# Graph transformer on one core: two value groups and two tail steps per turn beside the longest block

## Chip, cores and metric

The kernel runs on one core of a Trainium2 chip. The metric is the device time of one execution in microseconds (us); five executions of the kernel before gave 2874.62, 2865.3, 2837.87, 2857.81 and 2864.56, with a median of 2864.56. The core has five engines with instruction queues of their own: TensorE (PE, with its weight loads shown as PEld), VectorE (DVE), ScalarE (ACT), GpSimd (POOL) and SyncE (SP, which issues DMAs). Semaphores order them against each other; within one queue the work goes in the order in which it is written.

## What is computed

3327 nodes with 256 features, and a dense 0/1 adjacency of 3327 x 3327 in which a node has some 16 neighbours. Layer 0 averages over the neighbours, with softmax weights, and normalises. Then three layers, each of them the same graph transformer layer, sparse by the adjacency:

```python
qkv = layer_norm(x, g1, be1) @ w_qkv              # 8 heads of 32
scores = einsum('nhd,mhd->hnm', q, k) * SCALE
attn = softmax(where(adj != 0, scores, -inf))
out = einsum('hnm,mhd->nhd', attn, v).reshape(n, 256)
x = x + out @ w_proj + b_proj
h2 = layer_norm(x, g2, be2)
x = x + gelu(h2 @ w1 + b1) @ w2 + b2              # hidden width 1024
```

## The kernel before

Layer 0 works on the dense adjacency; on the way it sorts the nodes by their number of neighbours and lists the neighbours of each. It ends near 410 us and the change does not touch it. The three sparse layers (layer 1 to about 1275 us, layer 2 to 2082, layer 3 to the end) are what follows.

*Blocks and slots.* The nodes stand in 26 blocks of 128, one node to a partition. `CAPS[b]` says how many neighbours (slots) block b has room for: 34 in block 0, 23 and 22 in blocks 1 and 2, down to 9 in block 25. A slot of a block is one indirect DMA (L767, issued by GpSimd), which fetches the key and value rows of 128 neighbours. Up to `SG` = 4 slots form a group with one tile: block 0 has 9 groups, block 1 and block 2 have 6, block 25 has 3. Twelve such tiles exist (`SLOTS`), and gathers are sent up to `AHEAD` = 3 groups ahead of the scores.

*Order.* `ORDER` is 24, 23, ..., 1, 0, 25: blocks with few slots first, the longest (block 0) last but one, the shortest last. `CHUNKS` pairs them for the work behind the attention: [23,24], [21,22], ..., [3,4], [1,2], and block 0 and block 25 by themselves.

*The loop of a layer* (L879 on) goes through the blocks, k = 0 to 25, and through the groups g of each. One pass sends gathers, computes the scores of the group (`scores`: a product L781 and a sum L782 on DVE), after the last group also the maximum and the exponentials (`exps`, L788 to L792), then calls `turn()`. Then comes the block before: at g = 0 its softmax shares (`shares`, L798 to L800), and in each group as many of its value groups as `goal` says (`values`: a product L812 on DVE, then transposes on PE that sum up in `po`, L815). When all value groups of a chunk are through (a copy to oT on ACT, L821), the chunk's *tail* is opened. So the shares of block 0 and its value groups are written among the scores of block 25 (k = 25), and those of block 1 among the scores of block 0 (k = 24).

*A tail* is a generator, and `turn()` moves each open tail on by one step, the oldest first. Its steps, by lines: projection on PE (L666, L670; `pp`); add to x and variances on DVE (L673, L132 to L135); powers on POOL (L139); normalisation (L151 on DVE, L155 on ACT); transposes on PE and copy on ACT (L165, L167; `fT`); first half of the hidden layer on PE with gelu on ACT (L694, L698; `pu`); its products with the second matrix (L707; `pd`); second half of `pu`; second half of `pd`; add to x on DVE (L713) and variances; powers; normalisation; transposes (`hT`); and for each block of the chunk keys, values and queries of the next layer (L185 `pk`, L190 `pq`, copied by ACT at L187 and L192, and stored by SP at L729 and L730). The last layer has no such rows: after L713 the blocks are ready to be written to the output by POOL (L833). The list `hidden` lets one tail at a time into the MLP steps.

*At the end of a layer.* Beside block 25 (k = NB - 1, the last) `turn()` is called twice in a group. After the loop `turn()` goes on until no tail is left: the drain. The next layer's gathers wait for the stored rows of all blocks.

*What sets the order.* All of it stands under a manual schedule: each engine's queue holds the instructions in the order in which `layer` writes them. No planner changes it.

In the kernel before, chunk [3,4] is in its MLP beside the first groups of block 0; chunk [1,2] gets its projection beside block 0's group 6, its transposes and the first MLP steps beside block 25, and the rest in the drain together with the tails of [0] and [25].

Of the kernel before, what the change touches and what calls it, by code (L numbers as in the profile page):

```python
# [31 lines left out]
NB = (N + P - 1) // P  # L32
# [34 lines left out]
def kernel(ctx: ExitStack, tc: tile.TileContext, ins, out: bass.AP):  # L67
    nc = tc.nc

    def wt(L, name):  # L70
        return ins[f"L{L}_gnn_{name}"]
# [34 lines left out]
    def load_wq(L):  # L106
        t = wq_pool.tile([P, 2, 3 * D], FP, tag="wq", name=f"wq{L}")
        nc.scalar.dma_start(t, wt(L, "w_qkv").rearrange("(c p) n -> p c n", p=P))
        return t
# [87 lines left out]
    def node_rows(b):  # L197

        if b not in nodes_:
            nodes_[b] = lists.tile([P, NODE], FP, tag="node", bufs=NODES, name=f"node_{b}")  # L200
        nc.gpsimd.indirect_dma_start(
            out=nodes_[b], out_offset=None, in_=node_dr[:, :],
            in_offset=bass.IndirectOffsetOnAxis(ap=perm[:, b:b + 1], axis=0))
# [8 lines left out]
    def node_list(b):  # L212

        t = nodes_[b]
        cd = t[:, 2 * D:2 * D + CAND]
        nr = (CAPS[b] + 7) // 8
        w = 8 * nr

        cg = lists.tile([P, CAND], FP, tag="cg", bufs=2, name=f"cg_{b}")
        nc.vector.scalar_tensor_tensor(cg, cd, 0.0, segb.rearrange("p s k -> p (s k)"), ALU.is_gt, ALU.mult)  # L220
        nc.vector.tensor_add(cg, cg, cd)
        ls = lists.tile([P, LW], FP, tag="ls", bufs=2, name=f"ls_{b}")
        for k in range(nr):
            nc.vector.max(out=ls[:, 8 * k:8 * k + 8], in_=cg)
            if k < nr - 1:
                nc.vector.match_replace(out=cg, in_to_replace=ls[:, 8 * k:8 * k + 8], in_values=cg, imm_value=0.0)
        em = lists.tile([P, LW], FP, tag="em", bufs=2, name=f"em_{b}")
        own = lists.tile([P, 1], FP, tag="own", bufs=1, name=f"own_{b}")
        nc.vector.tensor_scalar(em[:, :w], ls[:, :w], 0.5, None, ALU.is_lt)
        nc.vector.tensor_scalar(own, pf[:, b:b + 1], 1.0, None, ALU.add)  # L230
        nc.vector.scalar_tensor_tensor(ls[:, :w], em[:, :w], own, ls[:, :w], ALU.mult, ALU.add)
        nc.vector.tensor_scalar(idx[:, b, :w], ls[:, :w], -1.0, None, ALU.add)
        nc.vector.tensor_scalar(bias[:, b, :w], em[:, :w], NEG, None, ALU.mult)
        nc.vector.tensor_reduce(found[:, b, 0:1], em[:, :w], AX.X, ALU.add)
        nc.scalar.copy(found[:, b, 1:2], t[:, 2 * D + CAND:])


    with ExitStack() as st:
# [51 lines left out]
        for L in LAYERS:  # L290
            o = 16 * (L - 1)
            for k, name in ((0, "g1"), (2, "be1"), (4, "g2"), (6, "be2"), (8, "b1")):
                n = wt(L, name).shape[0] // P
# [337 lines left out]
    with ExitStack() as st:  # L631
# [15 lines left out]
        def node_x(b):  # L647
            nc.scalar.copy(x_sb[:, b, :], nodes_[b][:, :D])

        def load_weights(L):  # L650
            w = {}
            for name, c, n in (("w_proj", 2, D), ("w1", 2, FF), ("w2", 8, D)):
                w[name] = wts.tile([P, c, n], FP, tag=name, name=f"{name}_{L}")
                nc.sync.dma_start(w[name], wt(L, name).rearrange("(c p) n -> p c n", p=P))
            return w
# [173 lines left out]
        def write(most):  # L829

            for b in ended[:most]:
                r = ROWS[b]
                nc.gpsimd.indirect_dma_start(  # L833
                    out=out, out_offset=bass.IndirectOffsetOnAxis(ap=perm[:r, b:b + 1], axis=0),
                    in_=x_sb[:r, b, :], in_offset=None)
            del ended[:most]

        def turn():

            for e in list(tails):  # L840
                e[0] -= 1
                if e[0] <= 0:
                    e[0] = next(e[1], None)
                    if e[0] is None:
                        tails.remove(e)

        def layer(L):
            w = load_weights(L)
            wqn = load_wq(L + 1) if L < LAYERS[-1] else None
            att = [Attend(L, b) for b in ORDER]  # L850
            todo = [(a, g) for a in att for g in range(len(a.cuts))]
            turns = len(todo)
            held = 0
            sent = 0
            oTs = {}
            left = [len(c) for c in CHUNKS]
            first = L == LAYERS[0]
            if first:
                for b in ORDER[:EARLY]:
                    node_rows(b)  # L860
                    node_x(b)
            att[0].load_q()
            att[0].place_q()
            att[1].load_q()
            att[1].place_q()
            before = None

            def part(a):

                m, j = place[a.b]  # L870
                if m not in oTs:
                    oTs[m] = work.tile([P, 2, 2 * P], FP, tag="oT", name=f"oT_{L}_{m}")
                if a.values(oTs[m], j):
                    left[m] -= 1
                    if not left[m]:
                        tails.append([1, tail(L, w, wqn, CHUNKS[m], oTs.pop(m))])

            now = 0
            for k, a in enumerate(att):  # L879
                n = len(a.cuts)  # L880
                if k + 2 < NB:
                    att[k + 2].load_q()
                for g in range(n):
                    if first and g == 0:
                        if k + EARLY < NB:
                            node_rows(ORDER[k + EARLY])
                        if EARLY <= k + 2 < NB:
                            node_list(ORDER[k + 2])
                            node_x(ORDER[k + 2])
                    while sent < turns and held < SLOTS and sent - now <= AHEAD:  # L890
                        todo[sent][0].gather(todo[sent][1])
                        sent += 1
                        held += 1
                    a.scores(g)
                    if g == n - 1:
                        a.exps()

                        if k + 2 < NB:
                            att[k + 2].place_q()
                    turn()  # L900
                    if k == NB - 1:
                        turn()
                    if sent == turns or len(ended) > LATE:
                        write(1)
                    if before is not None:
                        if g == 0:
                            before.shares()
                        goal = max(g + 1, -(-len(before.cuts) * (g + 1) // max(n - 1, 1)))
                        while before.vdone < min(goal, len(before.cuts)):
                            part(before)  # L910
                            held -= 1
                    now += 1
                before = a
            before.shares()
            while before.vdone < len(before.cuts):
                part(before)
                turn()
                write(1)
            while tails:
                turn()  # L920
                write(1)
            write(NB)

        with tc.manual_schedule():
            for L in LAYERS:
                layer(L)
# [190 lines left out]
```

## Time and profile before

| | us |
|---|---|
| median of 5 executions | 2864.56 (2837.87 to 2874.62) |
| profiled execution | 2858.64 |
| its span | 2856.8 |
| mean granted TensorE clock in it | 0.749 |
| layer 2: scores of block 0, group 1 (L781) | 1971.65 |
| layer 2: shares of block 0 (L798) | 2010.67 |
| layer 2: first `pu` of block 0, of block 25 | 2049.85, 2063.12 |
| layer 2: first gather of layer 3 | 2082.07 |
| layer 1: shares of block 0; first `pu` of block 0, of block 25 | 1202.73; 1242.99, 1256.26 |
| layer 3: shares of block 0; first `pu` of block 0, of block 25 | 2789.08; 2823.63, 2832.22 |

All times below the first line are of the profiled execution, counted from the start of its span. A line of a timeline reads: start, length, engine, line of the kernel, operation, output from inputs, shape, how many in a row, and in brackets how long the engine had been idle and who released it. "DVE L713 x_sb<-x_sb,pd [6.18 <-PE pd L707]" is the add that closes an MLP, which waited 6.18 us for PE. A group line of the page adds up all instructions of one line: count, busy us and mean ns, then the idle time just before them and what ended it.

### The profile page before, as it was taken

Reading aid. Unit: us, or ns where it says so; the run is one execution under the profiler, and the core shown is the slowest. Engines: PE = TensorE matmul, PEld = TensorE weight load, DVE = VectorE, ACT = ScalarE, POOL = GpSimd, SP = SyncE. Lnnn points to the kernel's source line nnn. Section 1 sums busy time; section 2 is a strip of 40 time slices with the busy share of each in tenths; the row PEclk is TensorE's granted clock in tenths of the full one; section 3 lists DMA queues with packets and bytes.
Section 4 is the critical chain, followed back from the end, with each engine's and each line's share of the span. In section 5 each row is a group of like instructions: output and inputs, shape, how many; then the busy total and the mean of one; then the engine's idle time right before and its main releaser. Section 6 shows DMA issues by size and latency. Waiting matters only on the chain.

```text
span 2856.8 us, 26111 instructions
## 1 busy us (share of the span) xinstructions
PE 1718.3 (60%) x8346; PEld 1331.5 (47%) x8346; DVE 1754.6 (61%) x3214; ACT 777.3 (27%) x1564; POOL 1430.6 (50%) x1614
## 2 busy tenths in 40 slices
PE   7677621455676666672556766766824556665656
PEld 6555411344554444451445544554613444454545
DVE  4877744676567776724654667657445757755573
ACT  4777510122332222230122222222311222111112
POOL 0232336565456665416554556656164656665562
PEclk8888855777787666795677878777956778676778
DMA  5667255455455664526554555656174655555561
GB/s 185 231 188 220 65 125 178 139 173 167 123 157 176 179 180 147 148 85 200 148 172 133 158 165 179 200 168 183 45 230 126 177 157 169 173 164 155 151 180 43
DMA packets 165083, 453.05 MB, mean 159 GB/s; under 512 B 37711, under 2 KB 64985, under 8 KB 161609
## 3 DMA queue, kind: packets, MB, share of 16 engines
q0 software_dynamic: 107104, 350.26, 41.8%
q1 hardware_dynamic: 56652, 98.53, 10.8%
q10 hardware_dynamic: 1180, 2.49, 0.3%
q8 instruction: 69, 1.13, 0.2%
q14 instruction: 78, 0.64, 0.1%
HBM read 410.86 MB, written 40.29 MB: 158 GB/s over the span
## 4 chain that ended last, share of the span: by engine, by line
PE 36%; another core or an unknown queue 16%; DVE 15%; issue 15%; ACT 6%; DMA 5%; POOL 5%; DVEq 0%; SPq 0%; ACTq 0%; POOLq 0%
PE pd L707 8%; PE pu L694 8%; PE po L815 6%; PE pk L185 5%; DVE sl L781 3%; POOL sl L767 3%; DVE sl L812 3%; PE pp L670 2%; PE pq L190 2%; DVE sc L782 2%; DMA sl<-kv,idx 2%; DMA kv<-kvr 1%; DMA node<-qr 1%; DVE cand L610 1%
## 5 line engine op out<-in xcount | busy, mean ns | idle before, releaser
L767 POOL DMA_INDIRECT sl<-kv,idx x1290 | 1228.9, 953 | 564.0 <-issue 358.6
L815 PE MATMUL po<-ident,sl 128*128 128x128 f32 x2580 | 470.2, 346 | 580.5 <-DVE sl L812 315.0
L815 PEld LDWEIGHTS po<-ident,sl 128*128 128x128 f32 x2580 | 396.0, 180 | 645.0 <-DVE sl L812 348.7
L781 DVE TENSOR_TENSOR sl<-sl,qw 128x1024 f32<-128x1024 f32 (+1 forms) x354 | 396.0, 1119 | 82.4 <-ACT qw L760 43.0
L782 DVE TENSOR_REDUCE sc<-sl 128x32 f32<-128x1024 f32 (+1 forms) x354 | 398.2, 1125 | 37.3 <-remote 20.1
L694 PE MATMUL pu<-fT,w 128*128 128x256 f32 (+1 forms) x1344 | 327.6, 401 | 137.5 <-ACT fT L167 89.3
L812 DVE TENSOR_TENSOR sl<-sl,qw 128x1024 f32<-128x1024 f32 (+1 forms) x354 | 388.9, 1119 | 9.1 <-remote 3.4
L707 PE MATMUL pd<-w,gT 128*128 128x256 f32 x1248 | 329.8, 421 | 107.2 <-ACT gT L698 73.1
L694 PEld LDWEIGHTS pu<-fT,w 128*128 128x128 f32 x1344 | 264.6, 212 | 186.5 <-ACT fT L167 93.6
L707 PEld LDWEIGHTS pd<-w,gT 128*128 128x128 f32 x1248 | 256.9, 212 | 166.0 <-ACT gT L698 85.6
L713 DVE TENSOR_TENSOR x_sb<-x_sb,pd 128x512 f32<-128x512 f32 (+1 forms) x42 | 27.2, 649 | 397.1 <-PE pd L707 338.1
L698 ACT ACTIVATE gT<-pu,pv 128x256 f32<-128x256 f32 (+1 forms) x336 | 133.5, 457 | 335.5 <-PE pu L694 170.3
L139 POOL TENSOR_TENSOR rsig_f<-rsig_f,mhalf 128x2 f32<-128x2 f32 (+1 forms) x42 | 29.1, 692 | 356.8 <-DVE rsig_f L135 341.7
L821 ACT COPY oT<-po 128x256 f32<-128x256 f32 x78 | 29.1, 373 | 629.3 <-remote 261.1
L673 DVE TENSOR_TENSOR x_sb<-x_sb,pp 128x512 f32<-128x512 f32 (+1 forms) x42 | 27.2, 649 | 269.0 <-PE pp L670 267.4
L185 PE MATMUL pk<-wq,hT 128*128 128x512 f32 x312 | 175.7, 692 | 22.8 <-ACT hT L167 22.3
L610 DVE MAX8 cand<-abf 128x8 f32<-128x256 bf16 x338 | 118.2, 410 | 0.6 <-DMA node<-cand 0.4
L167 ACT ACTIVATE fT<-pn_f,pv 128x256 f32<-128x256 f32 (+1 forms) x84 | 41.6, 546 | 258.5 <-remote 149.7
L670 PE MATMUL pp<-w_proj,oT 128*128 128x256 f32 x312 | 89.5, 434 | 36.7 <-ACT oT L821 26.7
L187 ACT COPY kvr<-pk 128x512 f32<-128x512 f32 x78 | 46.0, 590 | 199.9 <-PE pk L185 133.5
L185 PEld LDWEIGHTS pk<-wq,hT 128*128 128x128 f32 x312 | 63.6, 221 | 76.9 <-issue 41.3
L139 POOL TENSOR_TENSOR rsig_h<-rsig_h,mhalf 128x2 f32<-128x2 f32 (+1 forms) x28 | 19.4, 694 | 148.1 <-DVE rsig_h L135 118.1
(220 smaller groups left out, 2050.6 us busy)
## 6 DMA issues: line engine op xcount, KB each, us to landing
a<-in_adj_dram SPq DMA_DIRECT2D x25, 1663.5 KB
sl<-kv,idx POOLq DMA_INDIRECT x1290
kv<-kvr SPq DMA_DIRECT2D x78, 256.0 KB
q<-qr SPq DMA_DIRECT2D x52, 128.0 KB
q<-q SPq DMA_DIRECT2D x52, 128.0 KB
w<-in_L_gnn_w_dram SPq DMA_DIRECT2D x6, 1024.0 KB
node<-x SPq DMA_DIRECT2D x26, 128.0 KB
node<-qr SPq DMA_DIRECT2D x26, 128.0 KB
```

Of the source, the lines that this page charges most:

```text
L185: nc.tensor.matmul(pk, hT[:, c, :], wq[:, c, D:], start=(c == 0), stop=(c == 1))
L190: nc.tensor.matmul(pq[:, :D], hT[:, c, :], wq[:, c, :D], start=(c == 0), stop=(c == 1))
L610: nc.vector.max(out=cand[:, 8 * m:8 * m + 8], in_=ab3[:, m, :])
L670: nc.tensor.matmul(pp[:, j, :], oT[:, c, j * P:(j + 1) * P], w["w_proj"][:, c, :], start=False, stop=(c == 1 and j == n - 1))
L694: nc.tensor.matmul(pu[:, a, :n * P], w["w1"][:, c, f * P:(f + 1) * P], fT[:, c, :n * P], start=(c == 0), stop=(c == 1))
L698: nc.scalar.activation(gT[:, f0 + a, :n * P], pu[:, a, :n * P], AF.Gelu_apprx_tanh, bias=pv[:, L - 1, 8 + f:9 + f])
L707: nc.tensor.matmul(pd[:, j, :], gT[:, f, j * P:(j + 1) * P], w["w2"][:, h * FH + f, :], start=False, stop=(h == 1 and f == FH - 1 and j == ...
L767: nc.gpsimd.indirect_dma_start(out=t[:, k - a, :w], out_offset=None, in_=kv_dr[self.L][:, :], in_offset=bass.IndirectOffsetOnAxis(ap=idx[: ...
L781: nc.vector.tensor_mul(kq, kq, self.qp[:, None, :].to_broadcast([P, n, D]))
L782: nc.vector.tensor_reduce(self.sc[:, a:z, :], kq.rearrange("p s (h d) -> p s h d", h=HEADS), AX.X, ALU.add)
L812: nc.vector.tensor_mul(vv, vv, self.pw[:, a:z, :, None].to_broadcast([P, n, HEADS, HD]))
L815: nc.tensor.matmul(self.po[:, c, :], t[:, k, D + c * P:D + (c + 1) * P], ident, is_transpose=True, start=False, stop=(a + k == self.S - 1 ...
```

## The change

Two places in the loop of a layer. The second `turn()` in a group is called beside block 0 too (k = 24), not only beside block 25. And beside block 0 the goal of block 1's value groups counts two for each group of block 0, so that block 1's six value groups are written by block 0's group 2 instead of its group 5. It holds in all three layers; nothing else differs.

```diff
                     turn()
-                    if k == NB - 1:
+
+                    if k >= NB - 2:
                         turn()
                     if sent == turns or len(ended) > LATE:
                         write(1)
                     if before is not None:
                         if g == 0:
                             before.shares()
-                        goal = max(g + 1, -(-len(before.cuts) * (g + 1) // max(n - 1, 1)))
+                        h = (g + 1) * (2 if k == NB - 2 else 1)
+                        goal = max(h, -(-len(before.cuts) * h // max(n - 1, 1)))
                         while before.vdone < min(goal, len(before.cuts)):
                             part(before)
                             held -= 1
```

The order that follows on each engine, with the same instructions as before: the MLP of [3,4] beside groups 0 to 2 of block 0 (0 to 4 before), its rows for the next layer beside group 5; the projection of [1,2] beside group 3, its transposes and the first half of `pu` beside group 6, `pd` and the second half of `pu` beside group 7, the second half of `pd` and the closing add (L713) beside group 8. Powers to transposes of `hT` and the first rows of [1,2] come beside block 25, its last rows in the first turn of the drain. The tails of [0] and [25] begin where they did.

## The prediction

> **What bounds the kernel now.** I read the page from the top: busy shares, then the chain that ended last, then the groups.
>
> ```profile
> span 2856.8 us, 26111 instructions
> ...
> PE 1718.3 (60%) x8346; PEld 1331.5 (47%) x8346; DVE 1754.6 (61%) x3214; ACT 777.3 (27%) x1564; POOL 1430.6 (50%) x1614
> ...
> PE 36%; another core or an unknown queue 16%; DVE 15%; issue 15%; ACT 6%; DMA 5%; POOL 5%; DVEq 0%; SPq 0%; ACTq 0%; POOLq 0%
> ...
> L713 DVE TENSOR_TENSOR x_sb<-x_sb,pd 128x512 f32<-128x512 f32 (+1 forms) x42 | 27.2, 649 | 397.1 <-PE pd L707 338.1
> ```
>
> No engine is full. The last line counts most: before the 42 adds that close an MLP, VectorE (DVE) stood idle 397.1 us in all, 338.1 of them for pd. Each engine works in written order, so whatever is written behind such an add waits too.
>
> The change touches only the end of each of the three layers. I cut that end in three: A, the scores of block 0 (group 1 on); B, block 25's scores with block 0's values; C, the drain. The table of stretches for layer 2 (columns: length, then busy us and instructions of PE, PEld, DVE, ACT, POOL; granted clock, DMA share, GB/s):
>
> ```profile
> 1971.00:2011.00 40.00, 26.64 (x129) 20.66 (x127) 32.30 (x41) 9.06 (x17) 23.45 (x25) 0.84 0.58 170
> 2011.00:2026.00 15.00, 13.29 (x68) 9.04 (x68) 14.76 (x19) 4.74 (x10) 0.00 (x0) 0.85 0.16 54
> 2026.00:2082.00 56.00, 50.00 (x262) 38.74 (x260) 10.99 (x35) 21.80 (x53) 2.89 (x5) 1.00 0.09 31
> ```
>
> In A and B DVE is the fuller engine (32.30 of 40, 14.76 of 15), in C PE (50.00 of 56). PE is idle 13.4 us in A: room that seems to invite work from C. Whether it fits depends on when that work is ready, which the timeline of DVE shows:
>
> ```profile
> 1990.31 0.69 DVE L713 TENSOR_TENSOR x_sb<-x_sb,pd 128x512 f32<-128x512 f32 x1 [6.18 <-PE pd L707]
> ...
> 2002.63 0.69 DVE L673 TENSOR_TENSOR x_sb<-x_sb,pp 128x512 f32<-128x512 f32 x1 [0.82 <-issue]
> ...
> 2010.67 0.62 DVE L798 TENSOR_REDUCE sm<-sc 128x8 f32<-128x272 f32 x1
> ...
> 2045.96 0.69 DVE L713 TENSOR_TENSOR x_sb<-x_sb,pd 128x512 f32<-128x512 f32 x1 [7.84 <-PE pd L707]
> ```
>
> 1990.31 closes the MLP of chunk [3,4]. 2002.63 is the projection of chunk [1,2]; 2010.67 starts block 0's softmax shares, and with them B; 2045.96 closes the MLP of [1,2], and nothing but the drain stands behind it. PE's timeline gives that MLP's prices and, first, a matrix step after an idle stretch:
>
> ```profile
> 2011.67 3.78 PE L185 MATMUL pk<-wq,hT 128*128 128x512 f32 x4 [0.66 <-ACT hT L167]
> ...
> 2020.47 1.88 PE L185 MATMUL pk<-wq,hT 128*128 128x512 f32 x4
> ...
> 2028.48 3.62 PE L694 MATMUL pu<-fT,w 128*128 128x256 f32 x16
> ...
> 2033.62 3.72 PE L707 MATMUL pd<-w,gT 128*128 128x256 f32 x16
> ...
> 2042.30 3.62 PE L707 MATMUL pd<-w,gT 128*128 128x256 f32 x16
> ```
>
> **The change, part by part.** No instruction is added or removed; only their order moves. With two steps a turn beside block 0, the MLP of [1,2] is issued in block 0's groups 6 to 8 instead of in B and the drain. Its closing add (L713) now stands on DVE ahead of block 25's first scores, block 0's shares and all nine of block 0's value products (L812). That is a new wait in the middle of DVE's queue. I follow layer 2 with the durations of its own rows.
>
> 1. *MLP of [3,4].* Its four PE steps already run back to back, with 6 to 8 transposes between them; issuing them in groups 0 to 2 instead of 0 to 4 leaves the closing add at 1990.5 (1990.31 before). DVE has then one score group less done (1.9).
>
> 2. *Block 1's values, two groups a turn.* After add and variances (2.0) at 1992.5, the last two L812 (2 x 1.2, partly overlapping) end at 1994.7, their transposes at 1995.9, and the projection (0.4 copy, 0.60 + 3.06) at 1999.6: 3.0 us sooner than before. Add and variances: 2001.7.
>
> 3. *Query, key and value rows of [3,4].* One more score group (1.9) to 2003.6; normalisation, transposes and copy took 2.5 us from the ACT step to pk, so pk starts at 2006.5 against 2011.67. The two pk/pq pairs cost 4.7 (first one after idle) and 2.9: PE ends at 2014.1.
>
> 4. *MLP of [1,2].* On ACT its normalisation stands behind the row copies of [3,4]; from the end of pq to a finished fT took 3.0 us before (2023.2 to 2026.2). So pu starts at 2017.0. PE needs 3.62 + 0.38 + 3.72 + 3.62 + 3.62 = 15.0, with hand-overs to ACT 15.3: end at 2032.3. DVE has meanwhile done groups 5 to 8 and the maximum of block 0 (about 12 us, from 2003.6 to 2016) and waits some 16 us.
>
> 5. *Start of B.* Add and variances (2.0) and block 25's first scores (1.9): 2036.2 against 2010.67. **B starts 25.5 us later.** B itself (15.7 us of DVE work) is unchanged and ends at 2051.9.
>
> 6. *The drain.* Block 0's pu came at 2049.85, block 25's at 2063.12, after the MLP of [1,2] and its rows. Now the MLP is gone from there, but after B there still are on PE block 0's last transposes and projection (to 2052.2), hT (2053.3), two pk/pq pairs (2 x 2.9), block 25's transposes and projection (2.5 + 1.3), and the transposes for pu (1.0): pu of block 0 at 2063.8. From there to block 25's pu the undisturbed case is layer 3 (2823.63 to 2832.22, 8.6): 2072.4, or **9.3 later** than 2063.12. What follows is the same 17 us. C has given back 16.2 of the 25.5.
>
> Layer 1 has the same order (B starts 25.8 later): 9.3. Layer 3 has no rows for a next layer. Its closing add is at 2770.30 (0.7); then 7.1 to the end of the projection as in step 2, 2.0 for add and variances, two score groups (1.9, 2.4), 3.0 to fT, 15.3 for the MLP, 0.7 and 1.9 for the add and block 25's scores: shares at 2804.6, up to 0.8 for hand-overs, 2805.4 against 2789.08, 16.3 later. Block 0's pu follows B's end (2821.1) by about 8 (projection, add, variances, powers, normalisation, two hand-overs each way): 2829.2 against 2823.63, 5.6 later. Sum 9.3 + 9.3 + 5.6 = 24.2.
>
> **Costs that no row shows directly.** *Late hand-overs.* While gathers run, PE results sometimes reach ACT late: in layer 2's A, ACT waited 2.04 at 1986.89 with pu already done; in layer 3's A, pd began at 2754.47 after 8.88 us of idle PE. The moved MLP has four such hand-overs. From below 0 (they are at best on time), from above 8.9 a layer; I take 2, since layer 1 shows the same at 1178.25 (pu done by 1175.8), so 6 in all. *Clock.* That pd at 2754.47 took 6.18 for what takes 3.72 above; all four steps at that pace add 4 x 2.5 = 10 a layer, and the first pk pair at full pace would gain 1.9. I take neither: PE is busy nearly without a break from 2006.5. *GpSimd queue.* The powers (L139) of both chunks now stand ahead of the gathers of block 0's last groups and wait for the variances, some 5 us each. Gathers end near 2019 instead of 2004, still ahead of block 25's scores; without that cover each late group of four costs 5 us (4 x 1.25), and a gain isn't there, because the slots that come free sooner belong to gathers already ahead of DVE. *SP queue.* The row stores (L729, L730) go sooner; behind them stand only the next layer's loads, whose last condition stays block 25's rows: nothing. *ACT.* Block 0's exp comes behind the moved gelus with one table load (1.28) either way: nothing, as DVE is in its wait.
>
> 24.2 + 6 = 30 us on the profiled run of 2858.64 (span 2856.8): 2889. That run is 5.9 below the median 2864.56, against which the same sum gives 2895.
>
> The row 2011.67 (3.78 for what takes 1.88 at 2020.47) comes 1.8 us after a stretch in which PE did nothing for 7.24 us, and the pd of layer 3 after 8.88. [...]
>
> **Rivals.** *1, faster, 0.07.* The MLP hides in A. Break-even: C gives back 16.2, so the change gains if B starts before 2026.9 instead of 2036.2, which asks pu of [1,2] by 2007.7. For: PE's 13.4 idle us, and a total of some 92 us of PE work in the 110 from A to the end, so at most 18 a layer. Against: pu stands behind the two rows of [3,4] on PE and ACT. At 15 a layer: 2864.6 - 45 = 2820. *2, no change, 0.25.* Steps 3 and 4 go tighter (full clock at pk 1.9, the MLP's normalisation ahead of the second row copies 3, transposes overlapping 2), B is late by 16 to 19: 0 to 3 a layer, 2865 to 2874. *3, much slower, 0.15.* Late hand-overs as in layer 3 (8) or half pace in the MLP (10), in part both, in each layer: 24 + 3 x 14 = 66, around 2930. *The forecast, 0.53:* 2880 to 2912 by the bounds of hand-overs.
>
> **How the numbers follow.** Left out of the range are rival 1 and the upper half of rival 3, 0.15. Low 2862 is the foot of rival 2, high 2932 the middle of rival 3. A measurement here tells about 1% (29 us) from no change: faster 0.07; the forecast's 0.53 lies on both sides of 2893, 0.20 below and 0.33 above, so same is 0.25 + 0.20 = 0.45 and slower 0.33 + 0.15 = 0.48.
>
> **What would show it.** In the new trace: DVE idle 14 to 20 us before L713 of pd of [1,2], ahead of block 0's L798 (steps 4, 5); L798 16 to 28 us later after block 0's first scores; C shorter by some 16; projection of [1,2] some 3 sooner (2); gathers ending later but ahead of block 25's scores. Rival 1 would show L713 with an idle time under 6. I would be wrong if pu of [1,2] started before pk of [3,4] ends, or if the time before block 0 moved too.

## The result

The changed kernel takes 2885.21 us (median of 22 executions, 2865.64 to 2899.3) against 2856.61 for the kernel before (43 executions beside them). The ratio is **1.0096, 95% interval 1.0076 to 1.0115**: slower by 28.6 us by the medians (22 to 33 by the interval), where the sum of the prediction was 30.

The profiled execution has a span of 2867.9 us, 11.1 more than that of before. It hides part of the loss: block 0's first scores in layer 1 began 13.2 us sooner in it (1134.54 against 1147.71), ahead of the first moved instruction, and single executions of one kernel differ by as much. So I read the layers' ends by themselves. The page of the changed kernel, in the lines that answer to those shown of before:

```profile
span 2867.9 us, 26106 instructions
...
PE 1714.7 (60%) x8346; PEld 1326.8 (46%) x8346; DVE 1753.7 (61%) x3214; ACT 776.9 (27%) x1564; POOL 1430.8 (50%) x1614
...
L713 DVE TENSOR_TENSOR x_sb<-x_sb,pd 128x512 f32<-128x512 f32 (+1 forms) x42 | 27.3, 649 | 407.6 <-PE pd L707 328.6
```

The engines are busy for as long as before; the wait ahead of the closing adds grew by 10.5 us. DVE's timeline in layer 2 of the changed kernel (start, length, line, and in brackets the idle time ahead):

```profile
1978.18 0.69 DVE L713 TENSOR_TENSOR x_sb<-x_sb,pd 128x512 f32<-128x512 f32 x1 [9.74 <-PE pd L707]
...
1986.17 0.69 DVE L673 TENSOR_TENSOR x_sb<-x_sb,pp 128x512 f32<-128x512 f32 x1 [1.25 <-issue]
...
2001.59 0.44 DVE L791 TENSOR_TENSOR sc<-sc,mx 128x272 f32<-128x272 f32 x1
2018.60 0.69 DVE L713 TENSOR_TENSOR x_sb<-x_sb,pd 128x512 f32<-128x512 f32 x1 [16.57 <-PE pd L707]
...
2022.50 0.62 DVE L798 TENSOR_REDUCE sm<-sc 128x8 f32<-128x272 f32 x1
```

The second L713 is the closing add of [1,2]. DVE had block 0's scores ready at 2002.0 (L791) and then did nothing for 16.57 us, with block 0's shares (L798, 2022.50) behind that add. The table of stretches for the same layer, A, B and C (length; busy us of PE, PEld, DVE, ACT, POOL; clock, DMA share, GB/s):

```profile
1961.00:2022.00 61.00, 48.40 (x208) 35.97 (x207) 32.10 (x46) 14.74 (x32) 23.25 (x25) 0.92 0.39 119
2022.00:2038.00 16.00, 11.81 (x76) 10.51 (x77) 15.73 (x20) 1.46 (x3) 0.00 (x0) 0.79 0.01 1
2038.00:2077.00 39.00, 32.13 (x165) 23.28 (x163) 8.83 (x27) 16.85 (x41) 2.45 (x5) 1.00 0.14 48
```

PE's work in A rose from 26.64 to 48.40 us and fell in the drain from 50.00 to 32.13: the work did move. But A became 22 us longer for it, and the drain 17 shorter. With A from block 0's group 1 to its shares, B to block 25's maximum, C to the next layer's first gather (in layer 3 to the last write):

| | A before, after | B | C before, after | A to C |
|---|---|---|---|---|
| layer 1 | 41.89, 61.46 | 15.5 both | 57.27, 39.08 | +1.4 |
| layer 2 | 39.02, 61.17 | 15.5 both | 55.90, 38.74 | +5.0 |
| layer 3 | 45.99, 61.97 | 15.5, 15.4 | 40.57, 35.19 | +10.5 |

That is 16.9 us in this pair of executions, and 1.1 a layer more for the value group that now stands ahead of the start of A: 20 of the 28.6 that the medians show. One pair of executions can't settle the rest. Two later runs give a second pair: `whole` is the changed kernel again, and `add_34` takes as long as the kernel before. From A to C `whole` has 121.49, 116.39 and 116.88 us, `add_34` 109.68, 117.09 and 102.68. So a single layer differs by up to 7 us between two runs of a kind; the three layers together take 327 to 329 us in the one kind and 344 to 355 in the other, 15 to 28 more.

### The profile page after: what moved, and what is told of

It is laid out like the page before. It is cut to its first block, busy times and chain, and to the rows that moved or that the text cites. A ratio compares the mean times of both kernels' runs of the same rounds, so it can differ in the third digit from the quotient of the medians.

```text
span 2867.9 us, 26106 instructions
## 1 busy us (share of the span) xinstructions
PE 1714.7 (60%) x8346; PEld 1326.8 (46%) x8346; DVE 1753.7 (61%) x3214; ACT 776.9 (27%) x1564; POOL 1430.8 (50%) x1614
## 4 chain that ended last, share of the span: by engine, by line
PE 34%; another core or an unknown queue 19%; DVE 16%; issue 15%; ACT 7%; DMA 5%; POOL 4%; ACTq 0%; DVEq 0%; SPq 0%; POOLq 0%
PE pd L707 8%; PE pu L694 8%; PE po L815 5%; PE pk L185 4%; DVE sl L812 4%; DVE sl L781 3%; PE pp L670 3%; PE pq L190 2%; DVE sc L782 2%; DMA sl<-kv,idx 1%; POOL sl L767 1%; DMA kv<-kvr 1%; DMA out_dram<-x_sb,perm 1%; ACT gT L698 1%
## 5 line engine op out<-in xcount | busy, mean ns | idle before, releaser
L767 POOL DMA_INDIRECT sl<-kv,idx x1290 | 1229.1, 953 | 563.6 <-issue 362.1
L815 PE MATMUL po<-ident,sl 128*128 128x128 f32 x2580 | 473.4, 347 | 585.8 <-DVE sl L812 303.3
L815 PEld LDWEIGHTS po<-ident,sl 128*128 128x128 f32 x2580 | 397.9, 181 | 651.2 <-DVE sl L812 340.1
L781 DVE TENSOR_TENSOR sl<-sl,qw 128x1024 f32<-128x1024 f32 (+1 forms) x354 | 395.9, 1118 | 84.9 <-issue 44.3
L694 PE MATMUL pu<-fT,w 128*128 128x256 f32 (+1 forms) x1344 | 333.7, 404 | 152.0 <-ACT fT L167 100.8
L812 DVE TENSOR_TENSOR sl<-sl,qw 128x1024 f32<-128x1024 f32 (+1 forms) x354 | 388.2, 1119 | 8.9 <-remote 3.4
L707 PE MATMUL pd<-w,gT 128*128 128x256 f32 x1248 | 322.5, 415 | 99.6 <-ACT gT L698 80.0
L707 PEld LDWEIGHTS pd<-w,gT 128*128 128x128 f32 x1248 | 253.5, 209 | 157.0 <-ACT gT L698 92.5
L713 DVE TENSOR_TENSOR x_sb<-x_sb,pd 128x512 f32<-128x512 f32 (+1 forms) x42 | 27.3, 649 | 407.6 <-PE pd L707 328.6
L698 ACT ACTIVATE gT<-pu,pv 128x256 f32<-128x256 f32 (+1 forms) x336 | 133.0, 457 | 346.6 <-remote 165.9
L673 DVE TENSOR_TENSOR x_sb<-x_sb,pp 128x512 f32<-128x512 f32 (+1 forms) x42 | 27.3, 649 | 270.5 <-PE pp L670 267.4
L670 PE MATMUL pp<-w_proj,oT 128*128 128x256 f32 x312 | 89.5, 434 | 42.7 <-ACT oT L821 31.5
```

Of the source, the lines that this page charges most:

```text
L670: nc.tensor.matmul(pp[:, j, :], oT[:, c, j * P:(j + 1) * P], w["w_proj"][:, c, :], start=False, stop=(c == 1 and j == n - 1))
L694: nc.tensor.matmul(pu[:, a, :n * P], w["w1"][:, c, f * P:(f + 1) * P], fT[:, c, :n * P], start=(c == 0), stop=(c == 1))
L698: nc.scalar.activation(gT[:, f0 + a, :n * P], pu[:, a, :n * P], AF.Gelu_apprx_tanh, bias=pv[:, L - 1, 8 + f:9 + f])
L707: nc.tensor.matmul(pd[:, j, :], gT[:, f, j * P:(j + 1) * P], w["w2"][:, h * FH + f, :], start=False, stop=(h == 1 and f == FH - 1 and j == ...
L767: nc.gpsimd.indirect_dma_start(out=t[:, k - a, :w], out_offset=None, in_=kv_dr[self.L][:, :], in_offset=bass.IndirectOffsetOnAxis(ap=idx[: ...
L781: nc.vector.tensor_mul(kq, kq, self.qp[:, None, :].to_broadcast([P, n, D]))
```

## Experiments

Every comparison is with the kernel before on the same chip. One chip executes that kernel in 2355.55 us, the others in 2856 to 2881; ratios of the two kinds of chip are kept apart. The traces of before and of the changed kernel are of slower chips.

### Each half alone

Two turns, with the values as before (`turns_only`):

```diff
-                        h = (g + 1) * (2 if k == NB - 2 else 1)
+                        h = g + 1
```

> Two turns beside block 0, but block 1's values one group a turn as before. Theory (the closing add of [1,2] standing ahead of block 0's shares is what costs): [1,2] is opened three groups later, its add falls behind block 25's last scores, so DVE doesn't wait for it in A: DVE idle before L713 of [1,2] is in the drain again, shares of block 0 only 4 to 8 us later than before (the add of [3,4] comes two score groups sooner in DVE's queue), the drain shorter by as much or some us more; ratio 0.997 to 1.003. Rival 'each half carries its share' (the second turn itself costs, by moving work into the time of gathers): ratio 1.005 or more.

Two value groups, with one turn as before (`values_only`):

```diff
-                    if k >= NB - 2:
+                    if k == NB - 1:
                         turn()
```

> Block 1's values two groups a turn, but one turn beside block 0. Theory (the closing add): projection of [1,2] some 8 us sooner, its MLP on PE in B, its add behind block 25's last scores, no wait of DVE in A beyond the one for [3,4]; shares of block 0 within 2 us of before, drain 2 to 4 us shorter a layer; ratio 0.995 to 1.000. Rival 'each half carries its share': 1.003 or more, so that this and the other half sum up to the 1.0096 of the whole change.

On the faster chip (2355.55 before): turns alone **1.0118** (1.0093 to 1.0143), values alone **1.0055** (1.0032 to 1.0079). Both are on the side of the rival: each half costs. The whole change was not run on this chip, so whether the two sum up to it is open; they cost in different places. On this chip the run below with the change in layer 3 alone has layers 1 and 2 of before: A 37.25 and 36.86, C 56.06 and 55.79. With the turns alone A is 46.84 and 46.50, C 56.59 and 56.22: A pays 9.6 us and the drain gives nothing back, because the MLP of [1,2], opened three groups later, still runs beside block 25 and in the drain. What A pays, DVE's timeline shows:

```profile
1643.01 0.69 DVE L713 TENSOR_TENSOR x_sb<-x_sb,pd 128x512 f32<-128x512 f32 x1 [8.96 <-PE pd L707]
...
1664.14 0.69 DVE L673 TENSOR_TENSOR x_sb<-x_sb,pp 128x512 f32<-128x512 f32 x1 [5.46 <-PE pp L670]
```

The same two waits are 4.21 and 0.64 with one turn (layer 2 of the run with the change in layer 3 alone); the growth, 9.6 us, is what A pays. A second turn in a group writes each add to x one step nearer to the PE work that it needs, with less of DVE's own work between. With the values alone A is a little shorter (35.99, 36.02), and C 3.8 longer (59.85, 59.47).

### The change in layer 3 alone

```diff
-                    if k >= NB - 2:
+                    if k >= NB - (2 if L == LAYERS[-1] else 1):
...
-                        h = (g + 1) * (2 if k == NB - 2 else 1)
+                        h = (g + 1) * (2 if k == NB - 2 and L == LAYERS[-1] else 1)
```

> The whole change in layer 3 alone. By the prediction's sum (9.3, 9.3, 5.6) a quarter of the loss: ratio 1.0020 to 1.0025. By the two traces, A to end grows 1.4, 5.0 and 10.5 us in layers 1 to 3: most of the loss is layer 3's, ratio 1.0035 to 1.006.

**1.0017** (1.0000 to 1.0034) on the faster chip: as small as the prediction's sum has it. The 10.5 us of layer 3 in the pair of traces don't fit this ratio; they are of slower chips, where `whole` too has a long layer 3 (116.88 against 102.08 before). Layer 3 alone was not run there.

### The closing add out of the way

The changed kernel with L713 of [1,2] five turns later (`add_late`):

```diff
             hidden.remove(tag)
-            yield 1
+            yield 6 if b0 == 1 else 1
```

> The changed kernel, but the closing add of [1,2] (L713, with its variances) is written five turns later, behind block 25's last scores; the MLP on PE stays where the change put it. Theory (what is held behind that add on DVE costs): shares of block 0 come about 15 us sooner than in the changed kernel, PE's transposes of block 0 follow the MLP directly, so block 0's transposes end some 9 us sooner; the loss goes: ratio to before 0.996 to 1.000. Rival 'the MLP itself is slower beside the gathers (late hand-overs, lower clock)' or 'the second turn costs elsewhere': the ratio stays at 1.006 or more.

**1.0085** (1.0061 to 1.0110) on the faster chip: a miss. A is 55.33 and 55.21 in layers 1 and 2, still 18 more than the 37 of before. The trace of layer 2 says why. First DVE, then ACT:

```profile
1677.33 0.95 DVE L782 TENSOR_REDUCE sc<-sl 128x24 f32<-128x768 f32 x1
1692.51 0.64 DVE L798 TENSOR_REDUCE sm<-sc 128x8 f32<-128x272 f32 x1 [14.23 <-ACT sc L792]
```

```profile
1688.17 0.84 ACT L698 ACTIVATE gT<-pu,pv 128x256 f32<-128x256 f32 x2 [4.86 <-PE pu L694]
1689.90 0.84 ACT L698 ACTIVATE gT<-pu,pv 128x256 f32<-128x256 f32 x2 [0.89 <-PE pu L694]
1690.76 1.28 ACT L792 ACT_TABLE_LOAD   x1
1692.05 0.43 ACT L792 ACTIVATE sc<-sc 128x272 f32<-128x272 f32 x1
```

The add is gone from DVE's queue, and DVE waits all the same: now for block 0's exponentials (L792), which stand on ACT behind the gelus of [1,2] (L698), which wait for `pu` on PE. The MLP holds block 0's shares through two queues at once, and freeing one leaves the other.

### The exponentials out of the way too

As before, and the second half of `pu` with its gelus one turn later, behind the exponentials (`exp_first`):

```diff
                 if h == 0:
-                    yield 1
+                    yield 2 if b0 == 1 else 1
             hidden.remove(tag)
-            yield 1
+            yield 5 if b0 == 1 else 1
```

> As the run with the late add (the closing add of [1,2] behind block 25's last scores), and the second half of pu with its gelus one turn later, behind block 0's exponentials on ACT. Theory after the late add (the MLP holds block 0's shares twice: through the add on DVE, and through the gelus that stand ahead of the exponentials on ACT): shares of block 0 come some 8 us sooner than with the late add alone (DVE idle before L798 6 instead of 14.23 us), block 0's transposes end 4 to 5 us sooner (PE has to finish the MLP first), A to end some 111 us in layer 2 against 116.2 with the late add and 108.2 before; ratio 1.003 to 1.005. Rival (the second turn costs by itself, whatever stands ahead of the shares): no change against the late add, 1.008 or more.

And with the whole MLP of [1,2] behind the exponentials, both parts of the change left as they are (`mlp_after_exp`):

```diff
-            yield 1
+            yield 4 if b0 == 1 else 1
             pd = None
...
             hidden.remove(tag)
-            yield 1
+            yield 3 if b0 == 1 else 1
```

> Both parts of the change, but the MLP of [1,2] starts behind block 0's exponentials (block 0's group 8), and its closing add behind block 25's last scores: neither queue holds the shares back. Theory: shares of block 0 only 3 to 5 us later than before (the steps of [3,4] stand closer), no DVE idle above 3 us before L798; A to end 109 to 111.5 us in layer 2, what remains being the rows of [1,2], which now stand ahead of block 0's pu in the drain instead of inside its MLP; ratio 1.001 to 1.005. Rival (the second turn costs by itself): 1.008 or more.

The whole change, on the same chip as these two (`whole`):

> The whole change again, beside the runs that take parts of it away, on one chip. The chip of the last four runs executes the kernel before in about 2356 us instead of 2857 and shows no waits of ACT for finished PE work. If the loss is the order of the queues (MLP of [1,2] ahead of block 0's shares) and not late hand-overs, it must stay there: A some 20 us longer than before in layers 1 and 2, the drain some 17 shorter, ratio 1.006 to 1.010. If it came from late hand-overs beside the gathers (the 6 us of the prediction's sum and more), the ratio falls to 1.004 or less on such a chip.

It ran on a slower chip; what its expectation says of the faster one stays untested.

On a slower chip (2877.76 before): the whole change **1.0123** (1.0089 to 1.0157), the exponentials first **1.0047** (1.0018 to 1.0077), the MLP behind them **1.0039** (1.0011 to 1.0067). The same shares, block 0's in layer 2, in the run with the exponentials first and in the one with the MLP behind them:

```profile
2046.77 0.64 DVE L798 TENSOR_REDUCE sm<-sc 128x8 f32<-128x272 f32 x1 [7.14 <-ACT sc L792]
```

```profile
2029.72 0.65 DVE L798 TENSOR_REDUCE sm<-sc 128x8 f32<-128x272 f32 x1 [1.68 <-issue]
```

In layer 2 the wait falls from 14.23 with the late add (faster chip) to 7.14 and 1.68, in layer 1 from 14.16 to 12.01 and 6.89, where under 3 was expected. On the slower chip A in layer 2 falls from 62.16 (`whole`) to 50.19 to 44.91, and A to C from 116.39 to 110.30 to 109.80. PE ends the MLP of [1,2] about equally late in all three, 58.2, 58.0 and 57.9 us after the start of A (63.0, 62.5 and 64.3 in layer 1): the edits left PE's work where the change put it and freed only what stood behind it on DVE and ACT. So the shares held behind the MLP are the larger part of the loss, by the ratios some two thirds (1.0123 to 1.0039).

That the two end alike, though the shares come 5.3 us sooner in the second, PE's timeline explains. Layer 2 with the exponentials first, and with the MLP behind them:

```profile
2050.96 3.62 PE L707 MATMUL pd<-w,gT 128*128 128x256 f32 x16
...
2054.72 1.53 PE L815 MATMUL po<-ident,sl 128*128 128x128 f32 x12
```

```profile
2039.06 3.62 PE L707 MATMUL pd<-w,gT 128*128 128x256 f32 x16
...
2042.82 1.42 PE L815 MATMUL po<-ident,sl 128*128 128x128 f32 x11
```

Both times block 0's transposes (L815) stand behind the MLP's last product (L707), 58.1 and 58.0 us after the start of A. PE's queue is a third place where the MLP holds block 0. No run takes it away there, so what the remaining 0.4% consists of is open.

### Values alone, with the second half of pu later

> Only block 1's values two groups a turn (one turn beside block 0), with the second half of pu of [1,2] one turn later, behind block 25's exponentials on ACT. In the run with the values alone, ACT came to those exponentials only behind the gelus and the copy to oT (block 25's shares 20 us after its scores), PE stood idle 3.66 us for block 25's values, and the rows of [1,2] stood ahead of block 0's pu. Theory (queue order behind the MLP): here exponentials come at once, the rows of [1,2] fall back inside block 0's MLP, block 0's pu some 3.5 us sooner a layer than before; ratio 0.994 to 0.998. Rival (opening [1,2] sooner costs in any order): 1.002 or more.

```diff
                 if h == 0:
-                    yield 1
+                    yield 2 if b0 == 1 else 1
```

**1.0216** (1.0178 to 1.0254) on a slower chip, a clear miss. The values alone a second time, to part the chip from the edit:

> Block 1's values two groups a turn alone, a second time, beside the other runs of this call: 1.0055 on the faster chip, and the later variant of it 1.0216 on the slower one, where ACT began the gelus of [3,4] 4.6 and 10 us after PE had finished pu. If the chip makes that difference (PE's results reach ACT late beside gathers there), this run gives 1.003 to 1.008 on a fast chip, with DVE idle under 6 us before the add of [3,4], and 1.012 to 1.022 on a slow one, with idle times of 12 to 18 us. If the later second half of pu makes it, 1.003 to 1.008 on either.

**1.0145** (1.0117 to 1.0173), with 16.64, 17.91 and 23.45 us of idle DVE before the add of [3,4]. So the chip, not the later half, makes the values alone dearer, 1.0145 against 1.0055, and the later half of `pu` doesn't mend it: C is 62.48 and 62.00 with it, 60.20 and 60.38 without. My reading of why the values alone lengthen the drain (the exponentials of block 25 behind the gelus) falls with that; it stays open. What the slower chip does is seen on ACT in this second run, layer 2:

```profile
2007.17 0.84 ACT L698 ACTIVATE gT<-pu,pv 128x256 f32<-128x256 f32 x2 [14.19 <-remote]
2014.22 0.84 ACT L698 ACTIVATE gT<-pu,pv 128x256 f32<-128x256 f32 x2 [6.21 <-remote]
```

By PE's timeline of the run that `pu` was through at 2002.5. The gelus follow 4.7 and 11.7 us later. On the faster chip no such wait shows: the values alone have 18 waits of gT for "remote" here, 136.7 us in all, and three runs there (the turns alone, the late add, the change in layer 3 alone) have none.

### The closing add in the kernel before

The last question: does an add that stands too close behind its PE work cost time in the kernel before as well? First the add of [3,4] alone (`add_34`), then all adds that close an MLP (`add_all2`), then also the adds of the projection (`both_adds`):

```diff
             hidden.remove(tag)
-            yield 1
+            yield 3 if b0 == 3 else 1
```

> The kernel before, with the closing add of chunk [3,4] alone two turns later (behind block 0's group 6 instead of group 4). Theory: DVE's wait of 4 to 15 us before that add goes, A gets 4 to 8 us shorter a layer; the rows of [3,4] come later and stand in B, where PE has little room, so that the drain gets up to 4 us longer: ratio 0.993 to 0.999. Rival (PE sets the end from B on, and the rows of [3,4] are added to its queue there): 1.000 to 1.003.

```diff
             hidden.remove(tag)
-            yield 1
+            yield 2
             nc.vector.tensor_add(xi, xi, pd[:, :n, :])
```

> The kernel before, with the closing add of every MLP (L713) one turn later in all layers, so that one more score group and value group stand ahead of it on DVE; nothing else. Theory (an add written too close behind its MLP holds DVE's whole queue): DVE's idle time before L713, 397 us in the profile of before (206 in a run on the faster chip), falls by 80 us or more, and the kernel gets faster: ratio 0.96 to 0.99. Rival (outside a layer's end the gathers set the pace, so that the wait only moves to L781): idle before L713 falls, idle before L781 grows by as much, ratio 0.995 to 1.005.

```diff
-            yield 1
+            yield 2
             nc.vector.tensor_add(xi, xi, pp[:, :n, :])
...
             hidden.remove(tag)
-            yield 1
+            yield 2
```

> The kernel before, with both adds to x of every tail one turn later: the closing add of the MLP (L713, as in the run that gave 0.984) and the add of the projection (L673). With the first alone, DVE's idle time before L713 fell from 397 to 154 us, but before L673 it rose from 269 to 446, all of it waiting for pp. Theory (each add to x needs one more group of DVE work between itself and its PE step): idle before L673 falls by 150 us or more, ratio 0.94 to 0.975. Rival (the waits sum up to what PE and ACT need in a row for the tails, and move on to the next wait): idle moves to other lines, ratio 0.98 to 1.00.

The add of [3,4] alone: **0.9994** (0.9970 to 1.0018), no difference. DVE's wait before it shrank from 8.37, 6.18 and 14.73 us to 0.68, 2.31 and 3.38, but no gain shows in the time. All closing adds: **0.9840** (0.9805 to 0.9874). Both kinds: **0.9616** (0.9572 to 0.9659), 2747.78 us against 2856.41, faster than both kernels. The groups of the two adds (count, busy us, mean ns, idle time ahead), with the closing adds alone moved and with both:

```profile
L673 DVE TENSOR_TENSOR x_sb<-x_sb,pp 128x512 f32<-128x512 f32 (+1 forms) x42 | 27.3, 649 | 445.5 <-PE pp L670 445.2
L713 DVE TENSOR_TENSOR x_sb<-x_sb,pd 128x512 f32<-128x512 f32 (+1 forms) x42 | 27.1, 645 | 154.1 <-PE pd L707 114.3 <-remote 20.5 <-issue 13.8
```

```profile
L713 DVE TENSOR_TENSOR x_sb<-x_sb,pd 128x512 f32<-128x512 f32 (+1 forms) x42 | 27.1, 646 | 211.3 <-PE pd L707 145.4 <-issue 21.9 <-PE po L815 19.8
L673 DVE TENSOR_TENSOR x_sb<-x_sb,pp 128x512 f32<-128x512 f32 (+1 forms) x42 | 27.1, 645 | 51.8 <-remote 39.0 <-PE pp L670 7.6 <-PE po L815 5.3
```

In the profile of before, the two waits were 397.1 (L713) and 269.0 (L673). The first edit took 243 off the one and put 176.5 on the other; the second took both down to 263 together, 403 less than before. The time fell by 109, since part of the idle moved on: the wait before the shares (L798) rose from 91.1 to 383.4, of which 256.7 are put down to the exponentials on ACT, the second queue again. The gain lies in the middle of the layers (from the first gather of layer 2 to block 0's group 1: 645 us instead of 696), not at their ends (A to C 115.64 in layer 2, 110.42 before). Both edits also move all that follows the add in a tail one turn on, the MLP behind the projection among it, so the gain belongs to the wider spacing of the whole tail; it is not shown to come from the adds alone.

## Why the prediction was right, and where not

**The mechanism held.** DVE idle before the closing add of [1,2] was foretold at some 16 us, ahead of block 0's shares: 17.22, 16.57 and 11.12 in the three layers, the last below the 14 to 20 that were named. B was foretold unchanged: 15.5 before and after. The drain was to give back 16.2 in layer 2: 17.2 (18.2 in layer 1). That A loses more than C gives back is the result, and the runs that free the shares show that this wait is the larger part of it.

**The total is nearer than its terms.** Forecast were 9.3, 9.3 and 5.6 us for the layers and 6 for late hand-overs. The pair of traces has 2.5, 6.1 and 11.6 with the value groups, and the hand-overs are not shown. The misses partly cancel, so 30 against 28.6 is in part luck. Two slips didn't matter: the steps listed for layer 3 add up to 2805.3 and not 2804.6, within the 0.8 allowed behind them; and from block 25's pu to the next gather it takes some 19 us and not 17, but the sum used only that this stretch stays the same.

**Steps 1 to 3 were too slow.** From the start of A, the closing add of [3,4] came at 16.9 us instead of 18.9, the add of the projection at 24.8 (31.0 before, so 6.1 sooner where 3.0 were foretold), pk of [3,4] at 31.5 instead of 34.9. In layer 2 B therefore began 22 us later and not 25.5, 23.3 with the value group ahead of A. The 9.3 of layers 1 and 2 were 1.4 and 5.0 on these traces, 2.5 and 6.1 with that value group.

**Step 4 was right to 0.4 us in layer 2:** 14.94 from pu to the end of pd (2003.49 to 2018.43), 15.3 foretold, at full pace. Only the first pk and pq ran at half pace, 3.78 and 1.91 against 1.96 and 1.03 in the next pair (the first pk began 1.8 us after 4.83 us of idle PE), as in step 3. So the term for the clock was rightly left out there, and in layer 1 (15.1). In layer 3 no pk stands ahead of the MLP: its first pu began at 2784.54, behind 7.21 us of idle PE and four short transposes, and took 6.46 instead of 3.62, so that the MLP took 18.0. Of the 10 us a layer that the prediction named and left out, layer 3 paid 2.8. The gathers, later by then, still kept ahead of DVE: a single wait of 0.51 us in layer 2 (L781 at 1997.94).

**Layer 3 was mis-sized:** 5.6 foretold, 10.5 in the pair of traces (11.6 with the value group). The shares came 16.0 later (16.3), but the drain gave back 5.4 and not 10.7. GpSimd's queue holds a cost that the working left out: I had asked only what the gathers do behind the powers, and in layer 3 the output writes (L833) stand there too. GpSimd's timeline at the end of layer 3, before and changed:

```profile
2809.51 0.57 POOL L139 TENSOR_TENSOR rsig_f<-rsig_f,mhalf 128x1 f32<-128x1 f32 x1 [9.95 <-DVE rsig_f L135]
...
2842.61 2.56 POOL L833 DMA_INDIRECT out_dram<-x_sb,perm  x1 [2.39 <-DMA out_dram<-x_sb,perm]
```

```profile
2806.49 0.97 POOL L833 DMA_INDIRECT out_dram<-x_sb,perm  x1 [1.70 <-DMA out_dram<-x_sb,perm]
2822.34 0.57 POOL L139 TENSOR_TENSOR rsig_f<-rsig_f,mhalf 128x1 f32<-128x1 f32 x1 [14.88 <-DVE sm L798]
2823.11 1.03 POOL L833 DMA_INDIRECT out_dram<-x_sb,perm  x1 [0.20 <-issue]
...
2853.21 2.55 POOL L833 DMA_INDIRECT out_dram<-x_sb,perm  x1 [3.10 <-DMA out_dram<-x_sb,perm]
```

The powers of block 0 wait 14.88 us for its late variances (9.95 before), no write goes out meanwhile, and eleven writes, 2.7 us apart or more, stand between 2823.11 and 2853.21. The last came 5.9 us after block 25's add to x (2847.36); before it was 2.5 (2840.09 to 2842.61). So of the 10.5 us 3.3 are the writes; by the other 7.2 block 25's add itself came later after the start of A. With the change in layer 3 alone, on the faster chip, the loss was 4 us, 0 to 8, so the size stays uncertain.

**The ACT term was put at nothing for a reason that hid a cause.** "Nothing, as DVE is in its wait" was true for the sum. But it made the exponentials look harmless, and they were the second lock on the same door: with the add gone they kept A 18 us long.

**The late hand-overs, 6 us in the sum, are neither shown nor ruled out.** In the profiled execution the moved gelus of layer 2 were on time (pd waited 0.32 us). With the whole change on a slower chip, layer 1 had DVE idle 23.10 before that add, against 17.29 in layer 2. The whole change was not run on the faster chip, whose traces show none; with the late add, which leaves A 18 us long, it costs 0.85% there.

**A fuller A had a higher clock.** PE's mean granted clock in A of layer 2 was 0.92, against 0.84 before, with PE busy 48.40 us of 61 instead of 26.64 of 40. The time rose all the same: what ended A was block 0's shares, and the work that filled PE stood ahead of them.

Of the rivals, no change (0 to 3 a layer) is what layer 1 did on these traces; the faster one failed where the prediction put it: pu of [1,2] stood behind the rows of [3,4] and came 42.2 us after the start of A (2003.49), where break-even asked for 36.1. Of the much slower one only the 2.8 us of layer 3's first pu showed in this execution.

## What to carry to other kernels

Idle time of an engine is room for moved work only if every instruction behind that work, on every queue it passes through, can wait for it: list what stands behind its matmuls on TensorE, behind its add on VectorE, behind its gelus on ScalarE, behind its powers on GpSimd, and look for the critical one in all of them before taking out one. In a schedule written by hand, try giving an instruction that picks up another engine's result more of its own engine's work ahead of it; one turn more ahead of each such add, and of all that follows in its tail, gave 3.8% here. Where a wait is taken away and the time doesn't move, look where the idle time went.

## What was not expected of the hardware

The chips differ more than the kernels: 2355.55 us on one, 2856 to 2881 on the others, for the same kernel before, with the same durations of single instructions (953 ns for a gather's issue, L767, on both; 1119 and 1120 ns for L781; in B of layer 2 DVE is busy 14.76 us with 19 instructions and PE 13.29 with 68 on both). The difference is waits: DVE is busy 1754.6 us of 2856.8 in the kernel before and 1758.3 of 2356.5 on the faster chip (run with the change in layer 3 alone). PE differs too, 1718.3 us busy at a mean granted clock of 0.749 against 1622.2 at 0.802; which of the two brings the other about is not shown. The waits are plainest of ACT for PE. The table of waits on ACT, kernel before on the slower chip (line, releaser, total us, times, longest):

```profile
ACT oT L821 <- remote: 261.1, 14, 32.8
...
ACT fT L167 <- remote: 149.7, 10, 18.5
...
ACT gT L698 <- remote: 99.6, 14, 15.7
```

On the faster chip the same table has no line at all that ends in "remote"; oT waits 475.5 us there, all of it put down to PE, in 52 waits. Whether on the slower chips PE's last matmul ends late or its signal arrives late, the trace doesn't tell; it models the ends of matmuls.
